# Tokens kept in DRAM between two stages, fewer x buffers, and the sums over h in 64x64 tiles

## The chip, the core and the metric

The kernel runs on one core of a Trainium2 chip. The metric is the device time of one execution in microseconds; lower is better. The core has five engines with their own instruction streams: TensorE (PE; its weight loads are shown as PEld), VectorE (DVE), ScalarE (ACT), GpSimd (POOL) and SyncE (SP), which here issues nearly all DMAs. Each engine runs its stream in order and waits on semaphores for the others. SBUF is the on-chip memory, PSUM holds what TensorE writes, DRAM is off the core.

## What is computed

The input x has 32 images of 56 x 56 positions (w, h) and 96 channels. Two layers follow each other.

```python
# layer 0, a convolution block with mixed weights (rw from the mean of x)
pooled = mean(x, (1, 2));  rw = sigmoid(pooled @ Wr + br)
h = relu(bn(x @ mix(rw, Wpw)))          # 96 -> 384
h = relu(bn(depthwise3x3(h, mix(rw, Wdw))))
x = bn(h @ mix(rw, Wpwl)) + x           # 384 -> 96
# layer 1, on the 3136 tokens of an image
t = tokens(x)
h = relu(bn(layernorm(t) @ w1.T))       # 96 -> 192
y = irfft(nonlinearity(rfft(h over the tokens)))   # r, i, rb, ib per channel
t = t + bn(y @ w2.T)
t = t + ffn(layernorm(t))               # 96 -> 384 -> 96, rounded to fp8 / fp16
```

The transform over 3136 = 56 x 56 tokens is done in two steps of 56 as matrix products, with constant matrices dfta and dftb; dftc and dftd go back.

## The kernel before

All 32 images go through the same stages, and stages of neighbouring images are interleaved. Each stage is a Python generator ("stream") that names the engine it needs next and the events it waits for. A planner (`Plan`, `run`) keeps a model of the time of each engine, with a price for every operation (`Engine.issue`, `mm`, `transpose`, `arrives`), and at each step lets that stream go on which can start first; ties go by the priority given at `plan.spawn`. What comes out is a fixed order of instructions on every engine, written at build time. A PSUM tile comes from `psum(name)`, of which there are four. Where the planner sees TensorE idle for over 0.3 us before it, `psum` also writes up to 40 products of dftb with itself (line 321), "filler" whose result is overwritten; it keeps TensorE at work and computes nothing that is used.

The streams that matter here, for image b:

- `loads`: SP loads x[b] into one of three SBUF buffers `xpad`. It waits for the four output DMAs of image b - 3, which used the same buffer.
- `mixing`: VectorE sums x (pooled), TensorE makes the four router values (ps_rw), VectorE mixes wk (expansion), prod and small (biases and taps) and wk2 (projection).
- `expansion`, `convolved_tensor`, `convolved_vector`, `projection`: ps_pw, ps_dw (32x32 tiles of TensorE, 16 products at a time), h on VectorE, ps_pwl. `projected` adds the result to x in place; x then holds the tokens.
- `forward`, two streams of alternating strips (a strip is 14 columns of w, 784 tokens, as 7 pairs of columns): `moments` transposes the tokens (ps_t_a), takes bn_stats and makes rstd; ps_w<-w1c is the first product (96 rows, 112 tokens, 192 channels), `ha` its normalised relu on VectorE; ps_a sums over h with dfta (112 rows to 116 = 29 frequencies x 2 columns x re, im); ScalarE copies it to g, and SP stores g to DRAM (gd) in two DMAs.
- `frequency_loads`, `frequencies`, `nonlinearity`, `spectrum`: g is read back in another layout, summed over w with dftb (ps_b), passed through the nonlinearity, multiplied by w2 and dftc, and stored to DRAM (yd).
- `inverse`: SP loads yt, TensorE returns to tokens (ps_d), VectorE adds the result to x in place (`strip = xs[b][...]`); then the second layer norm, the two fp8 products (ps_f), the final sum on GpSimd, and the output DMA from the same x buffer.

So x[b] stays in its buffer from load to output.

```python
    xpad = [const([C, (S + 2) * S], F32, f"x_{i}") for i in range(min(3, NB))]
    ...
            yield SP, [("out", b - 3, s) for s in range(NS) if b >= 3]
```

Of the kernel before, what the change touches and what calls it, by code (L numbers as in the profile page):

```python
# [48 lines left out]
C = 96  # L49
# [7 lines left out]
PA = 4 * K1  # L57
KR = 2 * K1
# [3 lines left out]
SQ = SW // 2  # L62
T = SW * S
# [13 lines left out]
GK = 8  # L77
GROUPS = [(0, 16), (16, 13)]
# [52 lines left out]
class Plan:  # L131
# [8 lines left out]
    TAIL = {PE: 0.2, DVE: 0.12, ACT: 0.14, POOL: 0.1, SP: 0.0}  # L140

# [57 lines left out]
    def run(self):  # L199
        while self.streams:  # L200
            best = None
            for stream in self.streams:
# [14 lines left out]
                key = (max(ready, self.free[stream.engine]), stream.priority, ready)  # L217
# [68 lines left out]
def kernel(  # L286
# [39 lines left out]
    xpad = [const([C, (S + 2) * S], F32, f"x_{i}") for i in range(min(3, NB))]  # L326
    xs = [xpad[b % 3][:, S : S + N] for b in range(NB)]
    for b in range(min(3, NB)):
        nc.gpsimd.memset(xpad[b][:, 0:S], 0.0)
        nc.gpsimd.memset(xpad[b][:, S + N :], 0.0)  # L330
# [3 lines left out]
    nc.sync.dma_start(xs[0], x[0])  # L334
    prep = tc.tile_pool(name="prep", bufs=1)
# [14 lines left out]
    dfta_s = const([PB, NQ, PA], F32, "dfta_s")  # L350
    nc.sync.dma_start(dfta_s, dfta)
    dftb_s = const([PB, PB], F32, "dftb_s")
    nc.sync.dma_start(dftb_s, dftb)
# [6 lines left out]
    for kind in range(NKIND):  # L360
        at = 128 * kind
        while at < 128 * kind + 128:

            ch, p = at % CH, at - 128 * kind
            h, c = divmod(ch, C)
            n = min(C - c, 128 - p)
            nc.sync.dma_start(w2_s[p : p + n, kind, at // CH, :], w2t[c : c + n, h, :])
            nc.sync.dma_start(nl_s[p : p + n, :, kind], in_vecs[c : c + n, :, h])
            at += n
    dftc_s = const([PB, PB], F32, "dftc_s")  # L370
    nc.sync.dma_start(dftc_s, dftc)
    dftd_s = const([PA, NQ, PB], F32, "dftd_s")
    nc.sync.dma_start(dftd_s, dftd)

# [6 lines left out]
    nc.vector.tensor_add(ident32, ident32, ident[:, 96:128])  # L381
    ident8 = const([PB, PB], E5M2, "ident8")
# [117 lines left out]
    f1 = pp.tile([C, M], F32, tag="f1", name="f1")  # L500
    nc.sync.dma_start(f1, fw1t)
    nc.vector.tensor_copy(fw1, f1, saturate=False)
    f2 = pp.tile([128, NC3, C], F32, tag="f2", name="f2")
    nc.sync.dma_start(f2, fw2t)
# [10 lines left out]
    mixp = ctx.enter_context(tc.tile_pool(name="mix", bufs=2))  # L515
# [23 lines left out]
    plan = Plan(ps=4, mir=2, zo=1, h16=4)  # L539
# [22 lines left out]
    mixed, small_of, wk2s, gds, yds, zs = {}, {}, {}, {}, {}, {}  # L562


    def loads():
        for b in range(NB):
            yield SP, [("out", b - 3, s) for s in range(NS) if b >= 3]
# [74 lines left out]
    def expansion():  # L642

        for b, p, before in parts_of_all():
            xb = xpad[b % 3]
            for c in (2, 0, 1):

                for part, (at, ns) in enumerate((((0, (9, 9)), (18, (8, 8))), ((0, (8, 8)), (16, (9,))))[p]):
# [10 lines left out]
                    plan.spawn("evac pw", 5, expanded(b, p, c, part, at, ns, ps))  # L659
# [17 lines left out]
    def convolved_tensor():  # L677

        for b, p, before in parts_of_all():
            for i, wave in enumerate(WAVES[p]):  # L680
# [24 lines left out]
                plan.spawn("evac dw", 0, convolved(b, p, i, wave, ps))  # L705
# [41 lines left out]
    def projection():  # L747

        for b, p, _ in parts_of_all():
            needs = [("h2t", b, p, i) for i in range(len(WAVES[p]))] + [("wk2", b)]  # L750
            needs += [("h2v", b, p, c) for c, *_ in ON_VECTOR[p]]
            for s, blocks in (((0, (0, 1)), (1, (2, 3))), ((2, (4, 5)), (3, (6,))))[p]:
# [13 lines left out]
                plan.spawn("evac prj", 3, projected(b, s, blocks, ps))  # L766
            plan.done("prj", b, p)

    def projected(b, s, blocks, ps):
# [8 lines left out]
        plan.done("x1", b, s)  # L778

    def moments(name, xt, s, who, out, kept=None):  # L780
# [3 lines left out]
        for q in range(SQ):  # L784
            at = s * T + PB * q
            transpose(ps[:PB, 128 * q : 128 * q + C], xt[:, at : at + PB], ident[:C, :C])
        seen = slots(ps, PB, SQ, 128, C)
# [6 lines left out]

        st = sp.tile([PB, SQ, 6], F32, tag=f"st_{who}", name=f"st_{name}")
        for q in range(SQ):
            V.bn_stats(st[:, q, :], seen[:, q, :])
        if kept is None:
            plan.release()
        dm = sp.tile([PB, 2, SQ], F32, tag=f"dm_{who}", name=f"dm_{name}")  # L800
# [4 lines left out]
        W.behind.tensor_add(v, v, d)  # L805
        yield ACT
        rstd = sp.tile([PB, SQ], F32, tag=f"rstd_{who}", name=f"rstd_{name}")
        A.activation(rstd, v, AF.Sqrt, bias=eps_ln[:PB], scale=1.0 / C)
# [4 lines left out]
    def forward(parity):  # L813

        for b in range(NB):
            for s in range(parity, NS, 2):
                yield PE, [("x1", b, s)] + [("g2 read", b - 2)] * (b >= 2), 1
                if b not in gds:
                    gds[b] = dram.tile([PA, NQ, CH], F32, tag="gd", name=f"gd_{b}")
                xt, gd, got = xs[b], gds[b], []  # L820
                yield from moments(f"a_{b}_{s}", xt, s, f"a{parity}", got)
                rstd = got[1]
                for q0, nq in ((0, 4), (4, 3)):
                    yield PE, (), 1
                    ps = psum(f"ps_w1_{b}_{s}_{q0}")
                    for q in range(nq):
                        at = s * T + PB * (q0 + q)
                        mm(ps[:PB, 256 * q : 256 * q + CH], xt[:, at : at + PB], w1c)
                    yield DVE

                    ha = sp.tile([PB, 4, CH], F32, tag=f"ha{parity}", name=f"ha_{b}_{s}_{q0}")
                    for q in range(nq):
                        V.scalar_tensor_tensor(
                            ha[:, q, :],
                            ps[:PB, 256 * q : 256 * q + CH],
                            rstd[:, q0 + q : q0 + q + 1],
                            nshift[:PB],
# [6 lines left out]
                    for q in range(nq):  # L844
                        mm(ps[:PA, 256 * q : 256 * q + CH], dfta_s[:, s * SQ + q0 + q, :], ha[:, q, :])
                    yield ACT
                    g = sp.tile([PA, 4, CH], F32, tag=f"g{parity}", name=f"g_{b}_{s}_{q0}")
                    A.copy(g[:, 0:nq, :], slots(ps, PA, nq, 256, CH))
                    plan.release()
                    yield SP  # L850
                    at = s * SQ + q0
                    Q.dma_start(gd[0:PB, at : at + nq, :], g[0:PB, 0:nq, :])
                    Q.dma_start(gd[PB:PA, at : at + nq, :], g[PB:PA, 0:nq, :])
                arrives(4 * PA * 4 * CH, "g", b, s)
# [347 lines left out]
```

## Time and profile before

| | us |
|---|---|
| median of 3 runs | 4452.37 (4450.53 to 4455.45) |
| the profiled execution, its own time | 4452.19 |
| its span | 4450.0 |

| | stretch 0 to 62 us | 62 to 4300 | 4300 to 4450 |
|---|---|---|---|
| PE busy, us | 17.77 | 4130.74 | 135.93 |
| DVE busy, us | 34.56 | 3415.75 | 61.94 |
| ACT busy, us | 4.37 | 2546.10 | 76.10 |
| DMA share of 16 engines | 0.63 | 0.29 | 0.23 |

Busy time is the union of an engine's instructions. An fp32 product shows as two weight loads and two passes (MATMUL records), an fp8 product as one. A pass's end is modelled, so neighbours in time overlap in the records, and it is the distance of starts that tells the rate. The page's line for DMA gives 339.19 MB moved, 76 GB/s over the span.

### The profile page before, as it was taken

What the parts mean: (1) busy time and instruction counts of PE and PEld (TensorE: products, weight loads), DVE (VectorE), ACT (ScalarE), POOL (GpSimd) and SP (SyncE); (2) the same over time, 40 slices, a digit from 0 to 9 for tenths busy, and PEclk for the clock granted to TensorE, in tenths of its full rate; (3) what the DMA queues carried; (4) which work ended last, traced back from release to release, by engine and by line L of the source; (5) the groups of instructions that cost most, each with busy time, mean ns of one, the idle gap of its engine ahead of it and who ended that gap; (6) DMA issues with size and microseconds to landing.
All of it is one profiled execution on the core that took longest, in us unless ns stands there. A gap on an engine that the chain in (4) does not pass through costs nothing.

```text
span 4450.0 us, 114927 instructions
## 1 busy us (share of the span) xinstructions
PE 4284.4 (96%) x48916; PEld 3152.2 (71%) x48916; DVE 3512.3 (79%) x7222; ACT 2626.6 (59%) x4135; POOL 978.8 (22%) x1012
## 2 busy tenths in 40 slices
PE   6999999999999999999999999999999999999998
PEld 4767677677777677777677777677777777776778
DVE  6768787788877888778888778888788888778863
ACT  2455666655656565656565666556566656566654
POOL 1011222122222122222222222212222212222222
PEclk9999999999999999999999999999999999999999
DMA  3222332222332322332322332322332322332221
GB/s 91 55 65 64 81 91 78 72 75 71 81 83 71 87 71 75 81 83 71 87 69 73 85 83 71 87 70 67 90 80 72 82 65 76 93 80 71 76 77 49
DMA packets 305448, 339.19 MB, mean 76 GB/s; under 512 B 127908, under 2 KB 244452, under 8 KB 301636
## 3 DMA queue, kind: packets, MB, share of 16 engines
q1 hardware_dynamic: 304936, 331.85, 28.2%
q8 instruction: 384, 6.29, 0.6%
q14 instruction: 128, 1.05, 0.1%
HBM read 164.06 MB, written 158.27 MB: 72 GB/s over the span
## 4 chain that ended last, share of the span: by engine, by line
PE 67%; DVE 13%; ACT 8%; DMA 7%; issue 4%; POOL 1%; SPq 1%; POOLq 0%; ACTq 0%; DVEq 0%
PE ps_dw L553 14%; PE ps_pwl L553 11%; PE ps_w L553 11%; PE ps_pw L553 8%; PE ps_a L553 5%; DVE h L282 5%; PE ps_b L553 4%; PE ps_f L553 4%; DMA x<-in_x_dram 4%; PE ps_c L553 2%; DMA yd<-zo 2%; ACT z L282 2%; DVE z L282 2%; ACT mir L282 2%; PE ps_t_f L557 2%
## 5 line engine op out<-in xcount | busy, mean ns | idle before, releaser
L282 DVE SCALAR_TENSOR_TENSOR h<-hp,small,h 128x1792 f32<-128x1792 f32 (+2 forms) x768 | 1292.9, 1683 | 47.6 <-ACT h L282 31.8
L553 PE MATMUL ps_dw<-hp,diag 32*32 32x448 f32 x27648 | 858.7, 543 | 14.7 <-issue 14.6
L553 PEld LDWEIGHTS ps_dw<-hp,diag 32*32 32x32 f32 x27648 | 537.2, 103 | 281.7 <-issue 96.6
L282 POOL CAST h<-h 128x784 fp8e5<-128x784 f16 x384 | 382.6, 1022 | 1181.6 <-DVE h L282 1181.6
L553 PE MATMUL ps_pw<-x,wk 96*128 96x448 f32 (+1 forms) x1344 | 571.2, 564 | 34.5 <-DVE z L282 33.9
L553 PE MATMUL ps_pwl<-h,wk 128*96 128x448 f32 x1344 | 526.3, 539 | 0.0
L282 ACT ACTIVATE hp<-ps_pw,small 128x896 f32<-128x896 f32 (+2 forms) x384 | 361.3, 953 | 268.0 <-PE ps_pw L553 267.7
L282 ACT ACTIVATE nt<-yt,nm,rstd_f 112x96 fp8e5<-112x96 f32 x896 | 334.5, 454 | 201.0 <-DVE nm L282 200.8
L553 PEld LDWEIGHTS ps_pw<-x,wk 96*128 96x128 f32 x1344 | 244.6, 190 | 259.5 <-issue 186.5
L282 POOL TENSOR_TENSOR x<-x,y 96x784 f32<-96x784 f32 x128 | 286.8, 2241 | 551.2 <-DVE y L282 528.2
L553 PEld LDWEIGHTS ps_w<-w_s,z 128*112 128x112 f32 (+1 forms) x2816 | 361.5, 181 | 56.0 <-issue 48.4
L553 PE MATMUL ps_w<-w_s,z 128*112 128x96 f32 (+2 forms) x2816 | 376.7, 288 | 9.8 <-issue 9.2
L282 ACT ACTIVATE h<-ps_dw,small 128x448 f32<-128x448 f32 x384 | 214.9, 630 | 288.0 <-PE ps_dw L553 288.0
L553 PEld LDWEIGHTS ps_pwl<-h,wk 128*96 128x96 f32 x1344 | 209.5, 163 | 239.5 <-issue 228.5
L282 DVE SCALAR_TENSOR_TENSOR ha<-ps_w,rstd_a,nshift 112x192 f32<-112x192 f32 x896 | 308.2, 408 | 86.6 <-PE ps_w L553 86.6
L553 PEld LDWEIGHTS ps_b<-dftb_s,g 112*128 112x128 f32 x2816 | 334.8, 192 | 15.9 <-issue 13.2
L553 PE MATMUL ps_w<-w1c,x 96*112 96x192 f32 x1792 | 329.6, 329 | 9.9 <-ACT h L282 7.1
L553 PE MATMUL ps_b<-dftb_s,g 112*128 112x112 f32 x2816 | 339.0, 274 | 0.0
L553 PE MATMUL ps_a<-ha,dfta_s 112*116 112x192 f32 x1792 | 329.6, 330 | 7.7 <-ACT hp L282 7.4
L553 PEld LDWEIGHTS ps_a<-ha,dfta_s 112*116 112x116 f32 x1792 | 286.0, 181 | 36.5 <-ACT hp L282 31.0
L553 PEld LDWEIGHTS ps_w<-w1c,x 96*112 96x112 f32 x1792 | 284.6, 177 | 37.2 <-ACT h L282 18.9
L282 ACT ACTIVATE z<-ps_b,nl_s 128x448 f32<-128x448 f32 (+2 forms) x384 | 248.7, 689 | 88.3 <-PE ps_b L553 88.0
(160 smaller groups left out, 6197.7 us busy)
## 6 DMA issues: line engine op xcount, KB each, us to landing
gd<-g SPq DMA_DIRECT2D x128, 336.0 KB
g<-gd SPq DMA_DIRECT2D x32, 1344.0 KB
x<-in_x_dram SPq DMA_DIRECT2D x32, 1176.0 KB
yt<-yd SPq DMA_DIRECT2D x128, 294.0 KB
out_dram<-x SPq DMA_DIRECT2D x128, 294.0 KB
g<-gd SPq DMA_DIRECT2D x32, 1092.0 KB
gd<-g SPq DMA_DIRECT2D x128, 252.0 KB
yd<-zo SPq DMA_DIRECT2D x96, 336.0 KB
```

The costliest lines, as they stand in the source:

```text
L282: return getattr(self.namespace, name)(out, *args, **kw)
L553: nc.tensor.matmul(to, lhsT, rhs, start=start, stop=stop)
L557: nc.tensor.transpose(to, ap, eye)
```

## The change

1. Tokens. `projected` now also stores the tokens of its part to a DRAM tile (x1s, three of them). `inverse` no longer works in the x buffer: it loads each strip from that tile into one of four SBUF strips (tag x1), ahead of yt, and the output leaves from there.
2. x has two buffers. `loads` waits for image b - 2: its forward products ("x read") and its four token stores ("x1 by").
3. `forward` goes over the 28 column pairs in groups of 8, 8, 8 and 4 (FWD) in pieces of four. The first product is two products of 64 tokens each, in the two column halves of TensorE: 8 tokens ahead of each column and its 56, so that a column fills 64 PSUM rows. The sum over h is four products of 64 x 64 per two column pairs (dfta_s has zero rows for the 8). All 64 rows are copied, stored and kept in gd, in two DMAs of 64 partitions; g is loaded back in two DMAs of 56 partitions. dftb's rows are loaded in an order that undoes the swap of halves.
4. A product with a constant matrix `spread` puts the 112 variances into the 64-row positions (in the ps_t_a tile) before the square root.
5. Setup: f1 and f2 are loaded early, dfta and dftd late; w_s, nl_s and dftb are loaded through ScalarE's queue; GpSimd builds dfta_s from dfta_all.
6. The planner: new priorities, and a SLACK per engine in the choice of the next stream (0.2 us on VectorE, 1.2 on GpSimd).

```diff
+    SLACK = {PE: 0.05, DVE: 0.2, ACT: 0.1, POOL: 1.2, SP: 0.0}
...
-                key = (max(ready, self.free[stream.engine]), stream.priority, ready)
+                at = max(ready, self.free[stream.engine] + self.SLACK[stream.engine])
+                key = (at, stream.priority, ready)
...
-    xpad = [const([C, (S + 2) * S], F32, f"x_{i}") for i in range(min(3, NB))]
-    xs = [xpad[b % 3][:, S : S + N] for b in range(NB)]
+    xpad = [const([C, (S + 2) * S], F32, f"x_{i}") for i in range(2)]
+    xs = [xpad[b % 2][:, S : S + N] for b in range(NB)]
...
+    f1 = pp.tile([C, M], F32, tag="f1", name="f1")
+    nc.sync.dma_start(f1, fw1t)
+    f2 = pp.tile([128, NC3, C], F32, tag="f2", name="f2")
+    nc.sync.dma_start(f2, fw2t)
...
+    spread = const([PB, 2 * SP64], F32, "spread")
+    nc.gpsimd.memset(spread, 0.0)
+    for r in range(2):
+        at = SP64 * r + 8
+        nc.vector.tensor_copy(spread[:, at : at + S], ident[:PB, S * r : S * r + S])
...
+        nc.gpsimd.tensor_copy(
+            dfta_s[at, :, 0:KR].rearrange("p q (k i) -> p q k i", i=2),
+            dfta_all[at].rearrange("p q (k r i) -> p q k r i", r=2, i=2)[:, :, :, r, :],
+        )
...
-            yield SP, [("out", b - 3, s) for s in range(NS) if b >= 3]
+
+            yield SP, [(key, b - 2, s) for s in range(NS) for key in ("x read", "x1 by") if b >= 2]
...
+        if b not in x1s:
+            x1s[b] = dram.tile([C, N], F32, tag="x1", name=f"x1_{b}", bufs=3)
+        at = slice(blocks[0] * TB, (blocks[-1] + 1) * TB)
+        Q.dma_start(x1s[b][:, at], xs[b][:, at])
+        arrives(4 * C * n * TB, "x1 by", b, s)
...
+        if kept is None:
+            yield PE
+            np_ = 2 * SP64
+            mm(ps[:, C : C + n], spread, v)
+            v = ps[:, C : C + n]
...
-                    for q in range(nq):
-                        at = s * T + PB * (q0 + q)
-                        mm(ps[:PB, 256 * q : 256 * q + CH], xt[:, at : at + PB], w1c)
+                    for q in range(4):
+                        for r in range(2):
+
+                            at = S + PB * (lo + q0 + q) + S * r - 8
+                            mm(
+                                ps[SP64 * r : SP64 * r + SP64, 256 * q : 256 * q + CH],
+                                xpad[b % 2][:, at : at + SP64],
+                                w1c,
+                                share=2,
+                            )
...
-                    for q in range(nq):
-                        mm(ps[:PA, 256 * q : 256 * q + CH], dfta_s[:, s * SQ + q0 + q, :], ha[:, q, :])
+                    for q in range(0, 4, 2):
+                        for odd in range(2):
+                            for r in range(2):
+                                c = r ^ odd
+                                at = slice(SP64 * r, SP64 * r + SP64)
+                                to = 512 * odd + 128 * q
+                                mm(
+                                    ps[SP64 * c : SP64 * c + SP64, to : to + CH],
+                                    dfta_s[at, lo + q0 + q + odd, :],
+                                    ha[at, q + odd, :],
+                                    share=3.3,
+                                )
...
-                Q.dma_start(
-                    g2[:, 0:nk, :],
-                    gds[b][4 * k0 : 4 * (k0 + nk)].rearrange("(k a) q m -> (a q) k m", a=4),
-                )
+                for c in range(2):
+                    Q.dma_start(
+                        g2[S * c : S * c + S, 0:nk, :],
+                        gds[b][c, 2 * k0 : 2 * (k0 + nk)].rearrange("(k i) q m -> (i q) k m", i=2),
+                    )
...
-                yield SP, [("yd", b, i) for i in range(len(GROUPS))]
+                yield SP, [("yd", b, i) for i in range(len(GROUPS))] + [("x1 by", b, s) for s in range(NS)], "x1"
+                strip = sp.tile([C, T], F32, tag="x1", name=f"x1_{b}_{s}", bufs=NX1)
+                Q.dma_start(strip, x1s[b][:, s * T : s * T + T])
...
-            ("loads", 0, loads()), ("mixing", 5, mixing()), ("inverse", 3, inverse(0)),
-            ("inverse", 0, inverse(1)), ("frequency loads", 4, frequency_loads()),
-            ("frequencies", 3, frequencies()), ("forward", 2, forward(0)),
-            ("forward", 1, forward(1)), ("projection", 7, projection()),
-            ("vector", 8, convolved_vector()), ("tensor", 6, convolved_tensor()),
-            ("expansion", 9, expansion()),
+            ("loads", 8, loads()), ("mixing", 6, mixing()), ("inverse", 1, inverse(0)),
+            ("inverse", 0, inverse(1)), ("frequency loads", 0, frequency_loads()),
+            ("frequencies", 1, frequencies()), ("forward", 0, forward(0)),
+            ("forward", 0, forward(1)), ("projection", 7, projection()),
+            ("vector", 5, convolved_vector()), ("tensor", 2, convolved_tensor()),
+            ("expansion", 7, expansion()),
```

## The prediction

> **What bounds the kernel now.** I read the page's busy shares first, then TensorE's groups by form, then the waits, then one image's timeline on TensorE, VectorE and the DMA queue.
>
> ```profile
> PE 4284.4 (96%) x48916; PEld 3152.2 (71%) x48916; DVE 3512.3 (79%) x7222; ACT 2626.6 (59%) x4135; POOL 978.8 (22%) x1012
> ```
>
> TensorE stands at 96%, VectorE at 79%: a TensorE bound, it seems. But the groups by form (passes as count, busy us, mean ns) show that part of it is not work:
>
> ```profile
> L553 PE MATMUL ps_a<-ha,dfta_s 112*116 112x192 f32 x1792 | 329.6, 330 | 7.7 <-ACT hp L282 7.4 <-DVE ha L282 0.3
> L553 PE MATMUL ps_w<-w1c,x 96*112 96x192 f32 x1792 | 329.6, 329 | 9.9 <-ACT h L282 7.1
> L321 PE MATMUL ps_c<-dftb_s 112*112 112x112 f32 x794 | 96.5, 266 | 0.7 <-issue 0.7
> L321 PE MATMUL ps_w<-dftb_s 112*112 112x112 f32 x756 | 82.9, 265 | 0.3 <-DVE z L282 0.3
> L321 PE MATMUL ps_pw<-dftb_s 112*112 112x112 f32 x556 | 64.8, 274 | 0.0
> ```
>
> L321 is the filler that `psum()` writes where the plan sees TensorE idle. All L321 rows together hold 2,766 passes (an fp32 product is two passes, so 1,383 products) and 316 us: idle time that looks busy. Where it lies shows in the timeline of one image (start, length, group):
>
> ```profile
> 2126.01 0.37 PE L321 MATMUL ps_c<-dftb_s 112*112 112x112 f32 x2
> 2127.11 1.24 PE L321 MATMUL ps_c<-dftb_s 112*112 112x112 f32 x10 [0.73 <-issue]
> 2129.49 0.35 PE L553 MATMUL ps_rw<-wr_s,pool_b 96*128 96x4 f32 x2
> 2129.70 1.80 PE L321 MATMUL ps_w<-dftb_s 112*112 112x112 f32 x16
> 2133.49 1.16 PE L321 MATMUL ps_c<-dftb_s 112*112 112x112 f32 x10
> 2135.82 1.75 PE L321 MATMUL ps_pw<-dftb_s 112*112 112x112 f32 x16
> 2137.40 6.57 PE L553 MATMUL ps_pw<-x,wk 96*128 96x504 f32 x16
> ```
>
> The chain of waits and VectorE's timeline tell why:
>
> ```profile
> 2117.18 8.40 DMA x<-in_x_dram
> ```
>
> ```profile
> 2125.61 3.42 DVE L282 TENSOR_REDUCE pooled<-x 96x1 f32<-96x3136 f32 x1 [0.60 <-DMA x<-in_x_dram]
> 2133.95 1.92 DVE L282 SCALAR_TENSOR_TENSOR wk<-wpw_s,rw,wk 96x384 f32<-96x384 f32 x3
> ```
>
> The load of x for the next image starts only after the output of three images before has left the same buffer; it lands, is summed, mixed into wk, and only then can the expansion (ps_pw) begin. Each image pays some 10 us for this, as filler.
>
> [...] seven ps_n passes take 0.34 us before a full-array group (2065.15 to 2065.49), and 0.44 us before the 32x32 group (2043.03 to 2043.47): 0.10 us for the change. [...] 288 passes still take 8.73 us, 0.0303 us each, where a pass of the same 448 columns on the whole array (ps_pwl) takes 4.52/12 = 0.377 us. So 12.4 of 16 run together. [...] The new first product has two tiles with the same rows; no row of before shows that case.
>
> **The change part by part**, against the profiled execution: span 4450.0, its time 4452.19, 0.2 below the median of 4452.37. I add the same 2 us at the end.
>
> *Buffers and plan (tokens in DRAM, x load after forward, priorities).* In the built instruction streams, ps_rw of an image stands 14 rows before its first expansion in the kernel before (13 of them the rest of this wait) and 164 rows before it in the changed one, with a whole ps_dw wave of 8.7 us between. So x is off the path. The fillers fall from 1,383 products to 467. A filler pass takes 0.0985 us (2135.82 to 2137.40 for 16). 916 x 2 x 0.0985 = **-180 us**. What is late next: nothing that the plan sees, so part will return as real waits (below).
>
> *Startup.* Before, the chain waits for f2 behind dftd (18.08 us on the chain) and dfta, and ps_rw comes at 53.84 after 17.13 us of idle. In the new SP stream f1 and f2 stand ahead of both, and POOL's memset for rw no longer waits for them. POOL gets two copies of dfta_s (1,624 elements; the fp8 cast of 784 takes 1.02 us, so about 2 us each) behind that load, ahead of the diagonals: hidden, since the turned stk copies still come behind dftd. Bounds -25 and 0; I take **-17**.
>
> *Second product, ps_a, in four 64x64 tiles.* Before 896 products of two passes at 0.1625 us (16 passes from 2040.43 to 2043.03): 291 us. After 1,792 quarter products; all four together would be 1792 x 0.325 / 4 = 146 us; two together 291. The plan charges 0.33/3.3 = 0.10 us each. Its other prices hold in the trace (0.33 against 0.325 here; for ps_dw 0.0598 against 0.0606), so I take 179: **-112** (bounds -145 and 0). The groups, 224 of four columns, each change the mode in and, I assume, out: 224 x 0.20 = **+45**.
>
> *First product, ps_w<-w1c, in two 64-column halves.* 1,792 halves; paired, each costs 0.1625, in all 291 as before: 0. Mode changes again **+45** (bounds 0 and 45). Unpaired it is the rival below.
>
> *Spread.* 128 small products put the variances on 64-row positions. Like ps_rw, two passes: 0.2 us each, **+26**. They hold a PSUM buffer until the square root; that wait is planned and is in the filler count.
>
> *VectorE, ScalarE, GpSimd.* Operation counts stay (7,224 and 7,226 on VectorE), with 128 partitions for 112; ps_a is copied out in 224 pieces of 0.80 us instead of 256 that took 183.6 us. About 0. VectorE would stand at 3512/4280 = 82%.
>
> *DMA and SP.* Tokens go out and come back: 2 x 38.5 MB; 64 rows for 58 add 8 MB. 339 becomes 425 MB, 99 GB/s where slices of 93 occur already. g is now loaded in two DMAs of 56 partitions; [...] this load leads its readers, so I charge nothing. An issue holds SP 0.32 to 0.42 us; 244 more over 4,280 us are nothing by themselves. But a strip of 294 KB now stands ahead of every yt on SP, and waits for a free strip and its stored tokens; behind it stand gd, yd and wk. The plan expects strip plus yt in 1.4 + 613/220 = 4.2 us; x moved 1,204 KB in 8.40 us[...]. One late microsecond on one strip in four is **+33**; bounds 0 and 180, all that the fillers freed.
>
> Sum: -180 - 17 - 112 + 45 + 45 + 26 + 33 = -160; 4450 - 160 = 4290 span, 4292 with the 2 us, within the rounding of the terms. I forecast **4290 us**, its own range 4200 to 4360.
>
> **The rivals.**
> *Waits come back (20%).* The slack that filler stood for also absorbed late VectorE and DMA work. For it: every h row on VectorE runs longer than the plan's price (2.2 against 2.0 us at 1,792 elements), and TensorE already has small idle gaps (166 us in all). Against it: VectorE would still be idle 18%. If 110 us of 180 return: 4290 + 77 = 4367, up to 4440.
> *Tiles do better, strips come early (13%).* Four tiles together (-33), no drains on leaving (-45), nothing returned (-33): 4290 - 111 = 4179; with the drains on entering gone too (-45), 4134.
> *Column tiles don't run together: slower (12%).* If a half with the same rows must wait for the other's end, ps_w<-w1c takes 1792 x 0.325 = 582 (+291), and ps_a has only its two row tiles together, 291 (+112 over my 179): 4290 + 403 = 4693. [...] Against it: 12.4 of 16 in ps_dw needs columns together, too. It decides from 160/403, 40% of that loss; for ps_w alone from 0.09 us on top of 0.1625 a half.
> *The change doesn't free x (1%)*: then 4290 + 180 = 4470; the row counts above speak against it.
>
> **How the numbers follow.** Forecast's case 54%, waits 20%, better tiles 13%, columns serial 12%, x not freed 1%. The low end is the better tiles' bound, 4130; the high end takes in the returning waits, 4440; the serial columns are left out. A change within 0.2% (9 us, about what a measurement can tell from none) needs the middle of a broad span: 2%. Slower: 12% and the x case: 13%, faster 85%.
>
> **What would show it.** L321 rows with 934 passes in all; the chain without x's DMA; first ps_rw at 35 to 40 us; ps_a passes at about 0.05 us and ps_w<-w1c at 0.08 in a group's timeline; gaps of 0.1 us around both. Wrong if ps_w<-w1c halves stand 0.16 us apart, or if idle before ps_d (for yt) or other groups grows by over 100 us.

## The result and the profile after

| | before | after |
|---|---|---|
| median of 4 runs each, us | 4453.91 (4450.53 to 4456.15) | 4423.86 (4420.40 to 4426.14) |
| ratio | | 0.9933, 95% interval 0.9915 to 0.9950 |
| span of the profiled execution, us | 4450.0 | 4420.3 |
| mean granted clock of TensorE | 0.994 | 0.988 |

The granted clock is the share of its full speed that TensorE was given. The change is a gain of 0.67%; the prediction was 3.7%. The measured time lies within its widest bounds, 4130 to 4440 us, but above the 4200 to 4360 of its main case. The page of the changed kernel, its busy shares and its chain of waits by engine and by line:

```profile
PE 4143.1 (94%) x50924; PEld 2786.6 (63%) x50924; DVE 3481.1 (79%) x7224; ACT 2596.1 (59%) x4103; POOL 1097.7 (25%) x1015
PE 55%; DVE 18%; ACT 12%; DMA 8%; issue 4%; POOL 2%; SPq 0%; ACTq 0%; POOLq 0%; DVEq 0%
PE ps_w L585 11%; PE ps_dw L585 8%; PE ps_pwl L585 8%; DVE h L289 8%; PE ps_pw L585 8%; PE ps_b L585 6%; DMA g<-gd 5%; PE ps_d L585 4%; ACT nt L289 3%; ACT h L289 3%; DVE z L289 3%; DVE ha L289 3%; DMA gd<-g 2%; PE ps_f L585 2%; POOL h L289 2%
```

TensorE is busy 141 us less, the span shrinks by 30: the other 111 us are new idle time. x's load is off the chain, as foretold. In its place stand g's store and load, and VectorE.

TensorE's groups by form (passes as count, busy us, mean ns, idle before the group and who ended it), three of the kernel before and then the changed kernel's:

```profile
L553 PE MATMUL ps_b<-dftb_s,g 112*128 112x112 f32 x2816 | 339.0, 274 | 0.0
L553 PE MATMUL ps_f<-n,fw 96*128 96x392 fp8e5 x768 | 150.1, 329 | 4.4 <-ACT n L282 2.4 <-ACT h L282 1.9
L553 PE MATMUL ps_f<-h,fw 128*96 128x392 fp8e5 x768 | 150.3, 330 | 0.0
```

```profile
L585 PE MATMUL ps_b<-dftb_s,g 112*128 112x112 f32 x2816 | 372.0, 295 | 45.0 <-DMA g<-gd 37.5 <-ACT h L289 7.1 <-DVE z L289 0.4
L585 PE MATMUL ps_w<-w1c,x 96*64 96x192 f32 x3584 | 340.3, 332 | 2.4 <-ACT g L289 1.4 <-ACT rstd_a L289 0.8
L585 PE MATMUL ps_a<-ha,dfta_s 64*64 64x192 f32 x3584 | 197.5, 336 | 0.5 <-ACT h L289 0.2
L585 PE MATMUL ps_f<-n,fw 96*128 96x392 fp8e5 x768 | 178.9, 330 | 34.9 <-ACT h L289 15.4 <-DVE ha L289 12.8 <-ACT zo L289 5.6
L585 PE MATMUL ps_f<-h,fw 128*96 128x392 fp8e5 x768 | 151.5, 332 | 33.6 <-POOL h L289 32.0 <-issue 1.5
```

Twice the passes of ps_a take 197.5 us in place of 329.6; the halves of the first product take 340.3 in place of 329.6. So the tiles do run together. But ps_b now waits 45.0 us where it waited 0.0, and both ps_f groups wait 68.5 us together where they waited 4.4.

A stretch of TensorE's timeline (start, length, group) shows the tiles' pace:

```profile
2086.69 1.52 PE L585 MATMUL ps_w<-w1c,x 96*64 96x192 f32 x16
2088.15 0.54 PE L585 MATMUL ps_n<-ident,nt 112*96 112x112 fp8e5 x7
...
2090.51 0.88 PE L585 MATMUL ps_a<-ha,dfta_s 64*64 64x192 f32 x16
2091.32 1.52 PE L585 MATMUL ps_w<-w1c,x 96*64 96x192 f32 x16
```

From start to start, the 16 halves take 2088.15 - 2086.69 = 1.46 us and the 16 passes of the quarter products 2091.32 - 2090.51 = 0.81, changes of mode included. Eight whole passes of either took 8 x 0.1625 = 1.30 before.

The account of one image, from the times between one ps_rw and the next (mean of 22 images in the steady part with the same sequence of groups). "Work" is passes times the pace of each group where nothing holds it up, "filler" the passes of the filler line at 0.0985 us, "waits" the rest, time lost at a lower clock included:

| us an image | period | work | filler | waits |
|---|---|---|---|---|
| before | 133.96 | 122.00 | 5.71 | 6.25 |
| after | 132.99 | 120.18 | 0 | 12.81 |

Other sets of 22 neighbouring images give periods of 133.96 to 134.32 before and 132.96 to 133.27 after, so each row is good to some 0.3 us. The filler of the steady part is gone (5.71 x 32 = 183 us, the 180 of the prediction), and 6.56 us an image of new waits have taken its place. What is left, 0.97 us an image, times 32 is 31 us: the result. The two ends cancel: the changed kernel reaches its fifth ps_rw 58.7 us sooner (456.7 for 515.4), and after its last ps_rw it needs 61.6 us more (370.0 for 308.4), since ps_rw now stands earlier in an image's work.

### The profile page after: what moved, and what is told of

It is laid out like the page before. It is cut to its first block, busy times and chain, and to the rows that moved or that the text cites. A ratio compares the mean times of both kernels' runs of the same rounds, so it can differ in the third digit from the quotient of the medians.

```text
span 4420.3 us, 119618 instructions
## 1 busy us (share of the span) xinstructions
PE 4143.1 (94%) x50924; PEld 2786.6 (63%) x50924; DVE 3481.1 (79%) x7224; ACT 2596.1 (59%) x4103; POOL 1097.7 (25%) x1015
## 4 chain that ended last, share of the span: by engine, by line
PE 55%; DVE 18%; ACT 12%; DMA 8%; issue 4%; POOL 2%; SPq 0%; ACTq 0%; POOLq 0%; DVEq 0%
PE ps_w L585 11%; PE ps_dw L585 8%; PE ps_pwl L585 8%; DVE h L289 8%; PE ps_pw L585 8%; PE ps_b L585 6%; DMA g<-gd 5%; PE ps_d L585 4%; ACT nt L289 3%; ACT h L289 3%; DVE z L289 3%; DVE ha L289 3%; DMA gd<-g 2%; PE ps_f L585 2%; POOL h L289 2%
## 5 line engine op out<-in xcount | busy, mean ns | idle before, releaser
L289 DVE SCALAR_TENSOR_TENSOR h<-hp,small,h 128x1792 f32<-128x1792 f32 (+2 forms) x768 | 1318.1, 1716 | 56.9 <-ACT h L289 43.6
L585 PE MATMUL ps_dw<-hp,diag 32*32 32x448 f32 x27648 | 884.1, 545 | 31.5 <-issue 26.2
L289 POOL CAST h<-h 128x784 fp8e5<-128x784 f16 x384 | 544.5, 1443 | 1389.1 <-DVE h L289 1387.5
L585 PE MATMUL ps_b<-dftb_s,g 112*128 112x112 f32 x2816 | 372.0, 295 | 45.0 <-DMA g<-gd 37.5
L585 PE MATMUL ps_w<-w1c,x 96*64 96x192 f32 x3584 | 340.3, 332 | 2.4 <-ACT g L289 1.4
L289 ACT CAST h<-ps_f 128x784 f16<-128x784 f32 x384 | 292.7, 820 | 84.3 <-PE ps_f L585 81.8
L289 DVE SCALAR_TENSOR_TENSOR ha<-ps_w,rstd_a,nshift 128x192 f32<-128x192 f32 x896 | 309.7, 407 | 25.8 <-PE ps_w L585 21.5
L289 POOL TENSOR_TENSOR mir<-mir,z 128x448 f32<-128x448 f32 (+1 forms) x192 | 203.7, 1061 | 482.0 <-ACT mir L289 364.3
L289 POOL TENSOR_TENSOR x<-x,y 96x784 f32<-96x784 f32 x128 | 258.1, 2021 | 261.5 <-DVE y L289 261.5
L289 DVE SCALAR_TENSOR_TENSOR x<-ps_pwl,small,x 96x896 f32<-96x896 f32 (+1 forms) x128 | 131.5, 1027 | 209.2 <-PE ps_pwl L585 209.2
```

The lines of the kernel that those rows point to most:

```text
L289: return getattr(self.namespace, name)(out, *args, **kw)
L585: nc.tensor.matmul(to, lhsT, rhs, start=start, stop=stop)
```

## The experiments

Three explanations were tried first: A, the denser plan has no slack left, so waits stand where filler was; B, the added token transfers and x's load collide with g; C, the tile code itself brings the waits. Later letters are spelled out in the expectations. All ratios are to the kernel before, run on the same chip.

### Parts of the change, planned anew

Tiles alone (three buffers of x, tokens in place):

> The changed kernel with three x buffers again and the inverse working in place in x (no tokens in DRAM, no strips); tiles, planner priorities and setup as changed. Its stream has 1,653 filler products for 467, 234 us more at 0.197 us each. Theory A (the new waits come because the denser plan leaves engines no slack): the waits fall back from 12.8 us an image to about the 6.2 of before (-210 us), and the time is about 4424 + 234 - 210 = 4450, no different from before by more than 1%. Theory B (the waits come from the added DMAs of the tokens): the same, 4450, but the g load is quick again. Theory C (the tile code itself brings the waits, by its mode changes and longer PSUM holds): waits stay at 12 or so, time about 4650.

Measured 4933.34 us, ratio 1.1058 (1.1027 to 1.1089). The rest without the tiles:

> The kernel before with tokens in DRAM, two x buffers, four strips and the new priorities and SLACK, without the 64x64 tiles, the spread product and the new setup. 1,124 filler products. TensorE's own work is as before, 122 us an image without filler. Theory A: filler and waits trade, about 4424 to 4480. Theory B (the tokens' DMAs bring the waits): ps_b still waits for g and sits at 2 us or more an image, the total at 4450 or above. Theory C: waits at 6 an image, total near 3905 + 221 filler + 200 = 4330.

Measured 4643.35 us, ratio 1.0419 (1.0403 to 1.0434). The changed kernel with x's load held until g has come back:

```diff
-            yield SP, [(key, b - 2, s) for s in range(NS) for key in ("x read", "x1 by") if b >= 2]
+            yield SP, [(key, b - 2, s) for s in range(NS) for key in ("x read", "x1 by") if b >= 2] + [
+                ("g2 here", 2 * (b - 2))
+            ] * (b >= 2)
```

> The changed kernel; the load of x for image b also waits until the first g load of image b - 2 has landed, so it no longer stands ahead of the last gd stores and that load. 1,163 filler products. Theory B: the wait of ps_pw to ps_b (1.6 us), the half-clock ps_b (1.1) and part of the ps_dw stall (1.4) go, -100 us, against at most +137 of filler that the plan adds: 4400 to 4460, with the g load in 8 us for 11. Theory A: the g load is shorter, but the other waits (ps_f on ScalarE and GpSimd, 8 us an image) stay, and with the added filler the time is 4500 or more.

Measured 4902.80 us, ratio 1.0999 (1.0983 to 1.1015). And with measured prices in the planner (GpSimd's prices likewise):

```diff
-                us += n / 960.0
+                us += n / (860.0 if name == "scalar_tensor_tensor" and n > 800 else 960.0)
...
-        plan.done(*key, late=1.4 + nbytes / 220e3)
+        plan.done(*key, late=2.0 + nbytes / 145e3)
```

> The changed kernel planned with the durations that its trace shows: DMA 2.0 us plus 145 KB a us (for 1.4 and 220), GpSimd's cast 1.43 us (for 0.92), VectorE's long rows 2.2 us (for 2.0). Nothing else; it has 1,283 filler products. Theory A (the plan is too optimistic, so waits stand where no filler is): waits fall from 12.8 to under 8 us an image (-155), filler rises by 161: the time stays at 4400 to 4450, and clock windows at half rate become fewer. If it is over 4480, mispriced operations are not what brings the waits.

Measured 4702.30 us, ratio 1.0559 (1.0533 to 1.0585).

None of the four can be read for A, B or C: each edit changes events or prices, the planner then writes another order of everything, and all four orders are 4 to 11% slower, far above what was expected. The last two lie above the lines that their expectations drew (4500 and 4480 us), but as the order changed with them, that is not counted either. What the four show is that none of the orders planned with these priorities and this SLACK was good once something else had moved. Everything below keeps the planned order of every engine's instructions as it is, and changes only what is issued at a place.

### What a filler product costs

```diff
-            for _ in range(min(40, int((plan.idle() - 0.3) / 0.19))):
+            for _ in range(0 * min(40, int((plan.idle() - 0.3) / 0.19))):
```

> The kernel before with every instruction in its place and its 1,383 filler products left out (about 272 us of busy TensorE). The prediction's step says that this time stands on TensorE's path, so that less filler is less time: theory P, ratio 0.94 to 0.965. Theory A: the filler covers waits that are there anyway, so hardly anything is gained, ratio 0.985 to 1.000. Theory H: without it the clock is lower for part of the time, ratio above 1.000.

Measured 4477.74 us, ratio 1.0056 (1.0034 to 1.0079): 272 us less for TensorE to do, and slower. TensorE's waits in the kernel before, then in this one (us in total, times, longest):

```profile
PE ps_pw L553 <- DVE z L282: 33.9, 30, 1.4
...
PE ps_c L553 <- ACT zo L282: 13.3, 27, 2.0
...
PE ps_rw L553 <- DVE pool_b L282: 8.8, 15, 1.0
```

```profile
PE ps_c L553 <- ACT zo L282: 108.4, 66, 3.4
PE ps_pw L553 <- DVE z L282: 33.9, 30, 1.4
...
PE ps_w L553 <- DVE z L282: 13.1, 5, 5.5
PE ps_rw L553 <- DVE pool_b L282: 11.4, 17, 1.5
```

Where filler stood, TensorE now waits, above all for ScalarE's zo ahead of ps_c: 108.4 us in place of 13.3. The step behind x's load is not what holds it here: ps_rw's wait for pool_b, made from x's sum, grew only from 8.8 to 11.4 us, and ps_pw's for VectorE's z did not grow. The account of an image: period 134.46, work 122.00, filler 0, waits 12.46.

The filler had two uses. TensorE's idle time (span less busy time) rose from 165.6 to 338.4 us, 173 for the 272 of filler, so 64% of it was waiting. Its busy time fell by only 149 us (4284.4 to 4135.5), so the same work took some 123 us longer, and the granted clock fell from 0.994 to 0.965. Three runs with other amounts of filler show whether a smaller cut keeps more:

> The kernel before with every instruction in its place and 664 filler products in place of 1,383 (142 us of TensorE less), so that the clock may stay up where none of them left it down. Filler paid in full: ratio 0.966 to 0.972. Filler in time that is waited anyway: 0.995 to 1.003. A gain that the half clock took back when all filler went: between the two, 0.975 to 0.99.

> As the half-filler run, with 971 products (81 us of TensorE less than before). Filler paid in full: ratio 0.980 to 0.984. Filler in time that is waited anyway: 0.997 to 1.003.

> The kernel before with 1,675 filler products (57 us of TensorE more). Filler paid in full: ratio 1.011 to 1.015. Filler in time that is waited anyway, with time to spare: 0.998 to 1.004.

| filler products | clock | TensorE idle, us | ratio |
|---|---|---|---|
| 0 | 0.965 | 338.4 | 1.0056 (1.0034 to 1.0079) |
| 664 | 0.982 | 255.6 | 0.9989 (0.9981 to 0.9997) |
| 971 | 0.991 | 217.8 | 0.9963 (0.9951 to 0.9975) |
| 1,383 (before) | 0.994 | 165.6 | 1 |
| 1,675 | 0.994 | 151.1 | 1.0055 (1.0033 to 1.0077) |

The first 81 us taken out bring 0.0037 x 4452 = 16 us, a fifth of their length; the next 61 give 12 of it back, while the clock falls to 0.982. In all three cuts the same part comes back as idle time, 52 us of 81, 90 of 142 and 173 of 272; what is left is nearly used up, and in the end more than used up, by work at a lower clock. Added filler costs 24 us for 57. Nowhere is it paid in full. Why the first products are nearly free and the added ones less so was not followed further. The same for the changed kernel, whose 467 products stand at the start and the end:

> The changed kernel with every instruction in its place, but the 467 filler products on TensorE left out (they compute nothing that is used; about 92 us of busy TensorE). Theory A (the filler stands in time in which TensorE would have waited anyway): within 0.4% of the changed kernel, a ratio to the kernel before of 0.989 to 0.998. Theory P (TensorE is the bound and filler is paid for in full): the 92 us go, ratio 0.970 to 0.977. Theory H (the filler keeps the clock up): slower than the changed kernel, above 1.000.

Measured 4435.59 us, ratio 0.9964 (0.9952 to 0.9976), 0.3% above the changed kernel's 0.9933, with the clock at 0.978: theory A, with a little of H.

### Is TensorE's work paid at all?

In the kernel of the next part (g in one DMA), every group of ps_a was issued twice.

> The kernel with g in one DMA of 112 partitions, and each group of ps_a issued twice on TensorE (16 more passes in each of 224 groups, about 0.05 us each, 179 us or 5.6 an image). Theory P (TensorE's work is paid in full, so that the smaller ps_a was a real gain): ratio 1.010 to 1.016. Theory W (TensorE waits for the other engines anyway, and work in these places fills waits): 0.974 to 0.990.

```profile
L920 PE MATMUL ps_a<-ha,dfta_s 64*64 64x192 f32 x3584 | 186.4, 323 | 0.0
```

Measured 4407.16 us, ratio 0.9903 (0.9888 to 0.9918), against 0.9736 with ps_a once: 186 us more of TensorE's work cost 69 us (74 by the ratios), 37 to 40%. It lies on the edge of theory W: waits behind ps_a shrink (ps_f for GpSimd from 32.2 to 13.9 us).

### The load of g

The chain of waits of the changed kernel, one image (start, length, what):

```profile
2171.74 0.45 SPq L289
2172.19 0.04 issue
2172.23 4.09 DMA gd<-g
...
2176.37 11.03 DMA g<-gd
2187.40 0.14 issue
2187.53 7.21 PE ps_b L585 x48
```

and the timeline of SyncE and TensorE there:

```profile
2167.67 0.46 SPq L289 DMA_DIRECT2D x<-in_x_dram  x1
2171.74 1.08 SPq L289 DMA_DIRECT2D gd<-g  x2
2175.92 0.91 SPq L289 DMA_DIRECT2D g<-gd  x2
...
2187.53 7.21 PE L585 MATMUL ps_b<-dftb_s,g 112*128 112x112 f32 x48 [2.29 <-DMA g<-gd]
```

Two suspects stand in these lines: x's load of 1,176 KB, issued 4 us ahead of g's last stores, and the load of g itself, 11 us for 1,344 KB in two DMAs of 56 partitions. First, x's load behind g's:

```diff
-            if b:
+            if b > 1:
+                plan.tick(SP, 0.36)
+                held.append(b)
+            elif b:
                 Q.dma_start(xs[b], x[b])
...
+                send_held()
                 arrives(4 * PB * nk * CH, "g2 here", n)
```

> The changed kernel with every instruction of TensorE, VectorE, ScalarE and GpSimd in its place; on SyncE's queue alone x's load of the image after the next is issued after the first g load in place of ahead of gd's last stores and that load. Theory B (x's load collides with g's round trip): the chain's 11.0 us for g<-gd shrinks by 3 to 5 us, the wait at ps_b and the half clock behind it (1.6 + 1.1 us an image) go, ratio 0.974 to 0.984. Theory A: the wait only moves to another place, ratio 0.989 to 0.996.

Measured 4615.35 us, ratio 1.0368 (1.0344 to 1.0392): neither. Its chain says why:

```profile
1702.54 15.16 DMA x<-in_x_dram
1717.69 0.02 issue
1717.72 3.43 DVE pooled L289
...
1725.36 7.50 PE ps_pwl L585 x12
```

x now comes too late for its sum and stands on the chain again. Both loads have little slack, and x cannot wait until g has come. Then the load of g:

```diff
-                for c in range(2):
-                    Q.dma_start(
-                        g2[S * c : S * c + S, 0:nk, :],
-                        gds[b][c, 2 * k0 : 2 * (k0 + nk)].rearrange("(k i) q m -> (i q) k m", i=2),
-                    )
+                plan.tick(SP, 0.36)
+                Q.dma_start(
+                    g2[:, 0:nk, :],
+                    gds[b][2 * k0 : 2 * (k0 + nk)].rearrange("(k i) c q m -> (i c q) k m", i=2),
+                )
```

(gd is kept as 64 x 2 for 2 x 64, and dftb's rows follow. `plan.tick` books the time of the DMA that is no longer issued, so that the order stays.)

> The changed kernel with every instruction in its place, gd laid out so that g comes back in one DMA of 112 partitions in place of two of 56. If the two halves are slow [...], the 11.0 us of g<-gd become 9.5 to 10 and the ratio falls to 0.981 to 0.989; if they wait for the traffic around them, nothing moves, ratio 0.990 to 0.996.

Measured 4337.69 us, ratio 0.9736 (0.9717 to 0.9755), clock 0.997: 0.020 below the changed kernel, more than was expected. The same bytes in two DMAs of 112 partitions, split by k:

> As the run with g in one DMA of 112 partitions, but that load split by k into two DMAs of 112 partitions, so that there are as many DMAs as in the changed kernel. If the number of DMAs cost the 86 us, the time goes back to the changed kernel's, ratio 0.990 to 0.997. If it was that each DMA had only 56 partitions, it stays with the single load, ratio 0.971 to 0.979.

Measured 4323.02 us, ratio 0.9717 (0.9702 to 0.9731). It is not the number of DMAs, then, but their 56 partitions. TensorE's group ps_b there:

```profile
L585 PE MATMUL ps_b<-dftb_s,g 112*128 112x112 f32 x2816 | 335.4, 277 | 0.6 <-DVE z L289 0.4 <-ACT h L289 0.2
```

The wait is gone (45.0 to 0.6 us), and so are 37 us of busy time, ps_b's passes at a lower clock behind that wait (the granted clock rises from 0.988 to 0.997). The share of 16 DMA engines and the rate (the last two columns) while g comes in (the share adds up the time of all packets, so it can exceed 1), in the changed kernel,

```profile
2178.00:2180.00 2.00, 2.00 (x84) 1.16 (x64) 1.97 (x2) 0.00 (x0) 1.07 (x2) 1.00 0.97 215
2180.00:2182.00 2.00, 2.00 (x29) 1.23 (x11) 2.00 (x2) 1.06 (x1) 0.00 (x0) 1.00 0.98 170
2182.00:2184.00 2.00, 1.10 (x6) 0.50 (x5) 2.00 (x1) 2.00 (x4) 0.00 (x0) 1.00 0.98 180
```

and with two DMAs of 112 partitions:

```profile
2121.00:2123.00 2.00, 2.00 (x69) 0.98 (x62) 2.00 (x1) 0.00 (x0) 0.27 (x2) 1.00 1.10 310
2123.00:2125.00 2.00, 2.00 (x17) 1.39 (x12) 2.00 (x2) 1.86 (x2) 0.00 (x0) 1.00 1.11 233
```

A level of 0.98 against 1.11 is 0.88. The trace does not name the engines of a packet, so what lowers the level is not shown.

The lower level is the smaller part, though. A load of 1,344 KB is 1,792 packets of 768 bytes in all these kernels, and the packets of the traces give (medians over the 17 to 32 loads of a run that no other transfer of such packets touches; the rate is that of the load alone, in its middle part):

| load of 1,344 KB | issue to last packet, us | packets under way | one packet, ns | GB/s |
|---|---|---|---|---|
| before, one of 112 | 7.15 | 17.8 | 53 | 276 |
| before, two of 56 | 9.54 | 16.0 | 69 | 185 |
| after, two of 56 | 9.96 | 15.5 | 66 | 187 |
| after, one of 112 | 7.56 | 17.5 | 51 | 285 |
| after, two of 112 | 7.29 | 17.6 | 49 | 291 |

The packets under way fall to 0.88 (15.5 for 17.6), but each packet also takes a third longer (66 ns for 49), and that costs more. Why is not shown.

What the split costs in the kernel before (second row of the table), where the load has more lead over its readers:

> The kernel before with every instruction in its place and g loaded in two DMAs of 56 partitions in place of one of 112. The prediction charged this split nothing, since the load leads its readers. If that holds for the kernel before and only the changed order uses the lead up, ratio 0.998 to 1.003. If the split costs wherever it stands, about what it costs in the changed kernel: ratio 1.010 to 1.025.

```profile
L553 PE MATMUL ps_b<-dftb_s,g 112*128 112x112 f32 x2816 | 342.8, 276 | 24.9 <-DMA g<-gd 15.6 <-ACT hp L282 9.3
```

Measured 4487.59 us, ratio 1.0087 (1.0072 to 1.0102). Between the two cases: it costs 39 us even there, less than half of what it costs after. Here gd keeps its layout in DRAM, so it is the split that makes the load slow, not the layout that changed with it above. ps_b, which waited 0.0 us, now waits 24.9: about 2.4 us more of loading already use up the lead of the old order.

### The token traffic

> The changed kernel with every instruction in its place; the stores of tokens to DRAM and the loads of strips move 8 columns in place of 448 to 896, and the strips start at zero, so that the residual is left out. Theory B (the added token traffic delays g and TensorE's instruction fetch): the wait at ps_b and most of the 1.4 us an image in ps_dw go, ratio 0.970 to 0.982. Theory G (g is late for its own split and for the x load ahead of it): ratio 0.987 to 0.995.

Measured 4425.75 us, ratio 0.9944 (0.9927 to 0.9962), the changed kernel's own 0.9933 within the intervals. Moving the 2 x 38.5 MB of tokens costs nothing that can be measured: theory G. The DMAs themselves stay, with their issue and the events that the plan waits for, so their price is not in this run.

### The casts on GpSimd

What is left of the new waits is chiefly ps_f's. Both runs below issue GpSimd's cast with 8 of its 784 columns.

```diff
-        h = sp.tile([128, T], E5M2, tag=f"h8{parity}_{c}", name=f"h8_{b}_{s}_{c}")
-        P.tensor_copy(h, h16, saturate=False)
+        h = h8s[parity][c]
+        plan.tick(POOL, 0.1 + T * 1.04 / 1000.0, True)
+        nc.gpsimd.tensor_copy(h[:, 0:8], h16[:, 0:8], saturate=False)
```

> The kernel with g in two DMAs of 112 partitions, GpSimd's cast of the second layer's hidden values cut from 784 to 8 columns, so that most of these values are left out of the result. Theory C (the waits that took the filler's place are for GpSimd's casts, 32 us before ps_f, and for VectorE slowed beside them): 50 to 100 us go, ratio 0.948 to 0.961. Theory M (the same chain then waits at the next engine, ScalarE or VectorE): at most 20 us go, ratio 0.966 to 0.974.

> The kernel before with the same cut of GpSimd's casts, so that most of the second layer's hidden values are left out. In its profile ps_f<-h waits 0.0 us and casts take 1.02 us in place of 1.44. Theory C: the casts were covered there, ratio 0.995 to 1.001. Otherwise, if they slow VectorE in the kernel before too and VectorE sets the time: ratio below 0.99.

Measured 4272.52 us, ratio 0.9594 (0.9580 to 0.9609), against 0.9717 with the casts: 55 us. In the kernel before, 4463.82 us, 1.0021 (1.0010 to 1.0032): no gain. So the casts were covered, and are not in the new order: theory C of these two runs, at its small end. Groups of the changed kernel, then of the best order without casts, then of the kernel before without them:

```profile
L289 POOL CAST h<-h 128x784 fp8e5<-128x784 f16 x384 | 544.5, 1443 | 1389.1 <-DVE h L289 1387.5 <-PE ps_f L585 1.6
L289 DVE SCALAR_TENSOR_TENSOR h<-hp,small,h 128x1792 f32<-128x1792 f32 x256 | 579.0, 2262 | 7.9 <-ACT h L289 4.3
```

```profile
L1153 POOL CAST h<-h 128x8 fp8e5<-128x8 f16 x384 | 268.2, 698 | 1458.6 <-DVE h L289 1454.3 <-PE ps_f L590 2.2
L289 DVE SCALAR_TENSOR_TENSOR h<-hp,small,h 128x1792 f32<-128x1792 f32 x256 | 532.8, 2081 | 7.2 <-ACT h L289 3.6
L590 PE MATMUL ps_f<-h,fw 128*96 128x392 fp8e5 x768 | 146.5, 332 | 0.1
```

```profile
L1078 POOL CAST h<-h 128x8 fp8e5<-128x8 f16 x384 | 100.9, 271 | 1229.9 <-DVE h L282 1227.9
L282 DVE SCALAR_TENSOR_TENSOR h<-hp,small,h 128x1792 f32<-128x1792 f32 x256 | 569.5, 2225 | 9.0 <-ACT h L282 3.4
```

A cast of 8 columns takes 698 ns on the mean in the new order and 271 in the old one, so in the new order most of it is not the cast's own work. In the trace of the changed kernel, the 202 full casts that overlap one of VectorE's h rows (SCALAR_TENSOR_TENSOR) take 1,936 ns on the mean, and the other 182 take 896; of the h rows of 1,792 elements, the 87 that overlap a cast take 2,614 ns and the other 169 take 2,081. So the two run slower beside each other here; by what means is not shown. With less to cast, VectorE's h rows become 181 ns shorter (2,262 to 2,081); in the kernel before, where no row of 1,792 overlaps a cast, these take 2,225 ns with the casts and without. A full cast took 1,022 ns in the kernel before and takes 1,443 in the changed one: the new order lays more casts beside h (202 of 384, for 59).

The account of an image across the main runs:

| us an image | period | work | filler | waits |
|---|---|---|---|---|
| before | 133.96 | 122.00 | 5.71 | 6.25 |
| before, no filler | 134.46 | 122.00 | 0 | 12.46 |
| after | 132.99 | 120.18 | 0 | 12.81 |
| after, g in two of 112 | 129.95 | 120.18 | 0 | 9.77 |
| after, g in one of 112, ps_a twice | 132.50 | 125.85 | 0 | 6.65 |
| after, g in two of 112, no casts | 128.32 | 120.18 | 0 | 8.13 |

## Why the prediction was wrong

In the account of an image, times 32, the result is -183 for filler, -58 for work, +210 for new waits: -31, and the span shrank by 29.7. The prediction had -180, +4 and +33 for these, and -17 for the startup. Its own sign of being wrong came true: it named idle time before other groups grown by over 100 us, and TensorE has 111 us more.

**What comes back, +33: the step that failed.** The prediction counted the filler right (934 passes on the filler line) and booked its time as won, but for one late microsecond on one strip in four. What came back is 210 us. Under this step lay the reading that filler stood for x's load. In the kernel before without filler, TensorE waits 108.4 us for zo and 11.4 for pool_b: for the most part filler stood for other work of ScalarE and VectorE, and moving x's load does not shorten that. Taking filler out by itself brought at most a fifth of its length; 64% came back as waits, and much of the rest was lost at a lower clock. The change moved x's load off the chain, but let in other waits. The 210 us split up by the runs:

| new waits | us an image | times 32 |
|---|---|---|
| g in halves of 56 partitions (12.81 - 9.77) | 3.04 | 97 |
| GpSimd's casts beside VectorE (9.77 - 8.13) | 1.64 | 52 |
| the rest (8.13 - 6.25) | 1.88 | 60 |

The rival "waits come back" had the mechanism, and its 4367 to 4440 us hold the measured time. Its evidence, VectorE's h rows longer than the plan's price, does not come from the casts: cut, they leave these rows of the kernel before at 2,225 ns. Its 110 of 180 us is close to what the kernel with the mended load shows, (9.77 - 6.25) x 32 = 113, but nothing was worked out for it, so this is luck.

**The load of g, charged 0.** This is the largest part of that term. The prediction named the two DMAs of 56 partitions, and let the load lead its readers. In the new order it does not. With the load in two DMAs of 112 partitions, 0.9933 - 0.9717 = 0.0216 or 96 us go, and the kernel stands at 4323 us, 33 above the forecast. That it comes so near is luck in part: 80 us more of waits than foretold stand against better tiles.

**Tiles, -112 + 45 + 45 + 26 = +4.** Better than foretold: 0.81 and 1.45 us a group where 1.30 stood, so 7 groups of each in an image give 7 x (0.15 - 0.49) = -2.4 us, with +0.56 for spread -1.8, and -58 us over 32 images. The halves stand 0.09 us apart, not the 0.16 of the rival "column tiles don't run together", which is ruled out. The mode changes (the prediction's "drains"), charged at 90 us, fit into these numbers. What they cost is small here: for the halves, which save nothing, both changes come to 1.45 - 1.30 = 0.15 us if the halves pair in full. But work on TensorE is only paid in part (37% in the run with ps_a twice), so the whole 58 us need not have reached the time.

**Startup, -17.** The first ps_rw came at 47.37 us, 6.5 earlier, not at 35 to 40. Two things stand ahead of it: the product w1c, which VectorE releases 9 us later than before (36.27 for 27.10; what holds VectorE there was not tried), and 54 passes of filler from 39.21 to 47.37. In the changed kernel without filler the first ps_rw came at 39.62, inside the forecast, but its first ps_dw began no earlier for it (62.81 for 61.09). Whether the startup brought anything to the total is not shown.

**The strips themselves** cost little: ps_d waits 8.0 us for yt in place of 3.2, and moving the tokens costs nothing that can be measured.

**VectorE, ScalarE, GpSimd, about 0.** Their operation counts do stay, but GpSimd's casts grew from 382.6 to 544.5 us in the new order. This was not in the sum, and without the casts the best order is 55 us faster.

Open is the third row, and with it what sets the last 8.1 us of waits when the casts are gone: ps_w, ps_t_f and ps_f then wait for ScalarE's h and hp and VectorE's ha (32.7, 24.1 and 34.8 us in all, about 1 us an image each), and ps_dw is 1.7 us an image over its pace, where it was 0.9 over it before; none of these was taken away by itself.

The best kernel here is the changed one with g in two DMAs of 112 partitions: 4323.02 us, 0.9717 of the kernel before. One DMA of 112 can't be told from it (0.9736, the intervals overlap).

## What to carry to other kernels

Filler, or any busy time that computes nothing, can be a wait in disguise (64% of it here): before it is booked as a gain, ask which engine's chain the next real instruction would then wait for, and take the filler out of the old kernel with its order fixed to see its price, with the clock beside it. A transfer that "leads its readers" leads them by an amount that the change itself may use up: price its length in the new order, too. And where a planner writes the order, an experiment that lets it plan again measures another plan.

## What the runs showed of the hardware

A load of 1,344 KB took 9.96 us in two DMAs of 56 partitions and 7.29 in two of 112. The packets under way fell from 17.6 to 15.5, and one packet took 66 ns for 49; this was worth 2% of the time.

A wait cost more than its length. Behind the 2.29 us for g, ps_b's 48 passes took 7.21 us; at the 0.112 us a pass of an undisturbed group they would take 5.4. The stretch shows it in the column ahead of the last two, the granted clock:

```profile
2187.50:2194.70 7.20, 7.17 (x50) 7.20 (x50) 1.68 (x4) 3.57 (x6) 2.02 (x2) 0.76 0.87 255
```

A clock of 0.76 over 7.2 us comes to 0.24 x 2 x 7.2 = 3.5 us at half rate, and the clock records of this trace put the half rate at 2188.64, for 3.41 us: it set in 1.1 us after ps_b had begun. Ahead of that TensorE had waited 0.90 us, run a short ps_pw, and waited 2.29 us. How long a wait brings the half rate on was not shown. Over the whole span the records hold 60 us at half rate before and 111 after. The mean clocks of the other two runs give, as an estimate in the same way, 2 x (1 - 0.965) x 4473.9, some 310 us, without filler and 2 x (1 - 0.997) x 4320.1, some 26, with g in two DMAs of 112.
